# Triangle steps by a list of words, second residual in the accumulator, second norm's sums on ScalarE

## Chip, cores and metric

The kernel runs on one core of a Trainium2 chip. The metric is the device time of one execution in microseconds (us). TensorE is called PE in the profile, its weight load PEld, VectorE DVE, ScalarE ACT, GpSimd POOL, and the engine that issues most DMAs SP.

## The reference

Two layers on an input of 4 images with 64 x 64 tokens of 256 channels, all in fp32. The first is a self-attention over all 4096 tokens of an image. The second is a triangle attention, a norm, an MLP and a second norm. What the change touches is the second layer:

```python
def _L1_conv_ref(x_in, Wq, Wk, Wv1, Wv2, Wo, ln_agg_g, ln_agg_b, W1, b1, W2, b2, ln_out_g, ln_out_b):
    # ... q, k, v1, v2 = projections in 8 heads of 32
    scores = jnp.einsum('bilhd,bljhd->biljh', q, k) / np.sqrt(d_k)
    att = jax.nn.softmax(scores, axis=2)
    out = jnp.einsum('biljh,bilhd,bljhd->bijhd', att, v1, v2)
    attn_out = out.reshape(B, N, N, E) @ Wo
    h = x_in + attn_out
    h = _layer_norm(h, ln_agg_g, ln_agg_b)
    mlp = jax.nn.relu(h @ W1 + b1) @ W2 + b2
    h = mlp + h                                    # the second residual
    return _layer_norm(h, ln_out_g, ln_out_b)      # the second norm
```

## The kernel before

The program goes through the images one after the other. For each there is an attention stage, bound by TensorE, and a triangle stage of 32 steps. While the triangle stage of image b runs, the tokens of image b-1 (16 pieces of 256) are led through output projection, norm, MLP and norm: one piece per two steps. I call two steps and a piece a period. After the last image a tail does 15 pieces alone.

A step makes 8 products, some on DVE (`R`, three buffers) and some on POOL (`Rp`, two buffers), which TensorE sums into `acc`:

```python
def product(self, step, m):
    # ... npool(step) of the 8 products go to POOL: 3 in an even step, 2 in an odd one (b > 0)
    eng.tensor_tensor(R, src.unsqueeze(1).to_broadcast([P, D, N]), v2[:, h], ALU.mult)

def accumulate(self, step, m):
    for c in range(4):                             # four column groups of TensorE
        nc.tensor.matmul(acc[32 * c : 32 * c + 32, n % 2, :], w[:, n, c, 16 * h : 16 * h + 32],
                         R[:, ts(c, 8), :].rearrange("p d j -> p (d j)"), ...)
```

Second residual and second norm of a piece:

```python
def residue(self, tt):                             # POOL: z = h * gain + (shift + b2)
    h = self.h.pop(tt)
    z = self.z[tt] = work.tile([P, 2, C], F32, tag="s4", name="z")
    nc.gpsimd.tensor_tensor(z, h, lag_bc.unsqueeze(1).to_broadcast([P, 2, C]), ALU.mult)
    nc.gpsimd.tensor_tensor(z, z, lb2_bc.unsqueeze(1).to_broadcast([P, 2, C]), ALU.add)

def stats_o(self, tt):                             # DVE: add the MLP's output, then the statistics
    z = self.z[tt]
    nc.vector.tensor_tensor(z, self.zp.pop(tt), z, ALU.add)
    self.stats(z, 2)

def finish(self, tt, eng=nc.gpsimd):               # POOL: gain and shift of the second norm, store
    eng.tensor_tensor(z, z, log_bc.unsqueeze(1).to_broadcast([P, 2, C]), ALU.mult)
    eng.tensor_tensor(z, z, lob_bc.unsqueeze(1).to_broadcast([P, 2, C]), ALU.add)
    nc.sync.dma_start(...)
```

The order is a Python loop that writes one step after the other. Each engine runs its own queue in this order:

```python
for step in range(NSTEP):
    # ... (cut: conditions; loads, takes and stores of the step before)
    L.product(step, Q_[0]); L.product(step, D_[0])
    if odd: rest.polish(0 if odd_a else 2, 4, nc.gpsimd)
    if even_a: rest.heads(nxt, 0)
    L.accumulate(step, D_[0])
    next_weights()                                 # sums and weights of step + 1
    if odd_a: rest.affine_a(nxt)
    if odd: rest.affine_o(now)
    # ... (cut: products and sums between pieces of token work)
    if odd_a: rest.turn(nxt); rest.residue(nxt); mps = [rest.hidden(nxt, 0), rest.hidden(nxt, 1)]
    # ...
    if step % 2 == 0 and pair + 1 < NPAIR: L.scores(pair + 1, ig // 2)
    # ...
    if even: rest.stats_o(now); rest.roots(0 if even_a else 2, 4)
```

## Time and profile before

The median was 3938.9 us (3 runs). Stage borders are the first and last matmul into `acc`; the table is read from the busy times by stretch.

| part | us | PE busy | DVE | ACT | POOL |
|---|---|---|---|---|---|
| first triangle stage (no old tokens) | 430.6 | 383.8 | 394.6 | 236.4 | 396.9 |
| second | 489.5 | 451.6 | 452.1 | 258.7 | 461.2 |
| third | 490.8 | 453.0 | 452.3 | 258.9 | 461.2 |
| fourth (17 pieces) | 495.6 | 459.9 | 455.5 | 262.4 | 463.8 |
| tail | 174.2 | 153.9 | 108.3 | 81.1 | 76.0 |

The rest of the span of 3936.3 us are attention stages of 409 us, with some 38 us of start ahead of the first, and transitions of 43 to 46 us. No engine alone explains a triangle stage: three are busy 92 to 94% of it. Busy time of DVE and PE overlaps at instruction borders, so the prediction counts from start to next start ("by pace").

### The profile page before, as it was taken

To read this page: it belongs to the slowest core of one execution; us is meant where nothing else is said; L and a number is where in the kernel's file an instruction comes from. 1 tells how busy PE (TensorE), PEld (TensorE's weight loads), DVE (VectorE), ACT (ScalarE), POOL (GpSimd) and SP (SyncE) were. 2 spreads that over 40 slices of the span, in tenths; PEclk is the share of its full clock that TensorE was granted. 3 is DMA by queue.
4 is the path that set the end of the run, shared out by engine and by line. 5 is a ranking of instruction groups with operands and counts; after the bars stand their busy time and mean duration, and the time that the engine had idled before them with its cause. 6 is when DMAs were issued, how large, how long until landed. Compare 5 with 4: busy or idle time off the path is not lost.

```text
span 3936.3 us, 59354 instructions
## 1 busy us (share of the span) xinstructions
PE 3737.0 (95%) x23302; PEld 1742.6 (44%) x23302; DVE 2708.9 (69%) x2291; ACT 1814.4 (46%) x3775; POOL 1927.0 (49%) x1024
## 2 busy tenths in 40 slices
PE   9999998889999999998999999999899999999998
PEld 5444444433444444443344454444344444444376
DVE  4454499896444499998454459999644447999965
ACT  3333455554333455554333345555433335555544
POOL 4000098993000099998000049999500007999954
PEclk9999999999999999999999999999999999999999
DMA  4111445552111434323111154233211134331221
GB/s 119 50 51 48 116 139 137 136 144 96 49 51 51 121 74 91 84 53 87 52 51 46 54 131 93 55 85 74 75 48 47 49 99 103 84 85 45 53 70 50
DMA packets 439713, 309.38 MB, mean 79 GB/s; under 512 B 299328, under 2 KB 404544, under 8 KB 432128
## 3 DMA queue, kind: packets, MB, share of 16 engines
q1 hardware_dynamic: 419952, 291.12, 28.2%
q10 hardware_dynamic: 16240, 8.59, 0.8%
q0 software_dynamic: 3232, 5.78, 0.6%
q8 instruction: 186, 3.05, 0.3%
q14 instruction: 103, 0.84, 0.1%
HBM read 165.88 MB, written 139.46 MB: 78 GB/s over the span
## 4 chain that ended last, share of the span: by engine, by line
PE 72%; ACT 9%; DVE 6%; DMA 5%; POOL 3%; issue 3%; SPq 3%; ACTq 0%; POOLq 0%; DVEq 0%
PE o L432 24%; PE acc L808 12%; PE proj L489 8%; PE s L410 7%; PE mp L956 5%; PE zp L974 3%; DVE R L799 3%; PE sp L704 3%; PE v1p L514 3%; POOL Rp L799 2%; ACT S L714 2%; ACT ao L816 2%; SPq L823 2%; PE hp L863 2%; PE y L474 1%
## 5 line engine op out<-in xcount | busy, mean ns | idle before, releaser
L799 POOL TENSOR_TENSOR Rp<-attP,v 128x2048 f32<-128x2048 f32 x328 | 1490.1, 4569 | 449.9 <-DMA qk<-k 324.7
L799 DVE TENSOR_TENSOR R<-att,v 128x2048 f32<-128x2048 f32 x696 | 1547.3, 2273 | 95.4 <-PE acc L808 44.2
L439 DVE TENSOR_TENSOR esum<-esum,e 128x2048 f32<-128x2048 f32 x224 | 512.7, 2289 | 583.4 <-ACT e L421 580.5
L808 PE MATMUL acc<-R,wsel 128*32 128x512 f32 x5568 | 727.7, 605 | 64.3 <-DVE R L799 43.1
L421 ACT ACTIVATE e<-s 128x1024 f32<-128x1024 f32 x512 | 496.5, 1021 | 403.6 <-PE s L410 381.8
L902 POOL TENSOR_SCALAR nt<-mv 128x4 f32<-128x4 f32 (+1 forms) x51 | 9.9, 193 | 1283.6 <-DVE mv L880 1279.5
L816 ACT COPY ao<-acc 128x1024 f32<-128x1024 f32 x256 | 261.5, 1021 | 547.2 <-PE acc L808 436.2
L432 PE MATMUL o<-e,vlo 128*128 128x512 f32 x1024 | 473.7, 605 | 0.0
L432 PE MATMUL o<-e,vhi 128*128 128x512 f32 x1024 | 472.6, 605 | 0.0
L808 PE MATMUL acc<-Rp,wsel 128*32 128x512 f32 x2624 | 350.7, 610 | 35.1 <-POOL Rp L799 34.9
L808 PEld LDWEIGHTS acc<-R,wsel 128*32 128x32 f32 x5568 | 143.2, 109 | 396.0 <-issue 198.7
L432 PEld LDWEIGHTS o<-e,vlo 128*128 128x128 f32 x1024 | 184.0, 189 | 280.8 <-issue 280.8
L432 PEld LDWEIGHTS o<-e,vhi 128*128 128x128 f32 x1024 | 184.3, 189 | 279.7 <-issue 279.7
L410 PE MATMUL s<-gT,fT 32*128 32x512 f32 x2048 | 302.2, 640 | 4.8 <-ACT e L421 4.5
L956 PE MATMUL mp<-hT,w 128*128 128x256 f32 x1024 | 250.4, 390 | 39.6 <-ACT hT L936 39.6
L741 ACT ACTIVATE es<-S,rd 128x64 f32<-128x64 f32 x1024 | 258.4, 338 | 26.9 <-DVE rd L733 25.0
L451 DVE RECIPROCAL rec<-den 128x512 f32<-128x512 f32 x32 | 107.4, 3357 | 215.6 <-PE den L449 215.6
L974 PE MATMUL zp<-w,hid 128*128 128x256 f32 x1024 | 247.3, 387 | 2.9 <-ACT hid L963 2.9
L956 PEld LDWEIGHTS mp<-hT,w 128*128 128x128 f32 x1024 | 182.9, 189 | 117.4 <-ACT hT L936 57.8
L974 PEld LDWEIGHTS zp<-w,hid 128*128 128x128 f32 x1024 | 186.5, 191 | 67.5 <-issue 40.3
L501 ACT COPY st<-proj 128x512 f32<-128x512 f32 x104 | 60.9, 585 | 293.2 <-issue 165.9
L410 PEld LDWEIGHTS s<-gT,fT 32*128 32x128 f32 x2048 | 82.9, 182 | 193.7 <-issue 172.6
(153 smaller groups left out, 3795.3 us busy)
## 6 DMA issues: line engine op xcount, KB each, us to landing
v<-v2d SPq DMA_DIRECT2D x24, 1024.0 KB, 13.0
v1c<-v1d SPq DMA_DIRECT2D x128, 128.0 KB, 3.0
aT<-ao SPq DMA_DIRECT2D x1024, 16.0 KB, 1.9
A<-aT SPq DMA_DIRECT2D x256, 64.0 KB, 2.1
out_dram<-z SPq DMA_DIRECT2D x63, 256.0 KB, 2.2
y<-yT SPq DMA_DIRECT2D x56, 256.0 KB, 2.0
q<-st SPq DMA_DIRECT2D x56, 256.0 KB, 2.6
v1d<-st SPq DMA_DIRECT2D x56, 256.0 KB, 2.2
```

The costliest lines, as they stand in the source:

```text
L410: nc.tensor.matmul(s_ps[r // 2][:, r % 2, :], fT[rows, tt, ts(n, P)], gT[rows, ts(qb, QB)], start=True, stop=not safe,)
L421: nc.scalar.activation(e[g][:, 2 * j : 2 * j + 2, :], s_ps[j], AF.Exp)
L432: nc.tensor.matmul(o_ps[qb], F.v[tt][:, r * 4 + n, :], es[:, r, :], start=(k == 0 and r == 0), stop=(k == 7 and r == 3),)
L439: nc.vector.tensor_tensor(esum[qb], esum[qb], es, ALU.add)
L489: nc.tensor.matmul(ps, w[:, cc, rows], y(qb, cc), start=(cc == 0), stop=(cc == 1))
L514: nc.tensor.matmul(ps[:, ts(n, C)], y(qb, cc)[:, ts(m * 2 + n, P)], wv1_sb[:, cc, :], start=(cc == 0), stop=(cc == 1),)
L741: nc.scalar.mul(self.e[:, i, :], rows[:, i, :], rec[:, i : i + 1])
L799: eng.tensor_tensor(R, src.unsqueeze(1).to_broadcast([P, D, N]), v2[:, h], ALU.mult)
L808: nc.tensor.matmul(acc[32 * c : 32 * c + 32, n % 2, :], w[:, n, c, 16 * h : 16 * h + 32], R[:, ts(c, 8), :].rearrange("p d j -> p (d j)"), ...
L816: nc.scalar.copy(self.ao[step][:, ts(np, 2)].rearrange("p k d j -> p k (d j)"), acc)
L956: nc.tensor.matmul(self.mp[:, fc % 2, :], w1_sb[:, cc, ts(fc, P)], self.hT[tt][:, cc, :], start=(cc == 0), stop=(cc == 1),)
L974: nc.tensor.matmul(zp[:, n, :], self.hid[tt][:, fc, ts(n, P)], w2_sb[:, fc, :], start=(fc == 0), stop=(fc == 3),)
```

## The change

Three things are changed. The intent of the first is to take the second residual off POOL and DVE: TensorE transposes `h` anyway; a second copy of that transposed tile, with the shift and b2 in its bias, is transposed back by TensorE into the accumulator of the MLP's output. The second takes the second norm's statistics to ScalarE, whose activations can give a sum. The third writes the later triangle stages from a list of words; "/1" behind a word is by how many periods it is late, so what belongs to one step is spread over up to three periods. In a word, R is a product, A a sum into `acc`, T the copy of an accumulator, E and O the even and odd step.

```diff
+ORDER = """
+    r0/1 AO0/2 AO1/2 m1/1 RO4/2 RE5/1 SO/1 RO5/2 TO0/2 sp/1 AO4/2 AO6/2 r1/1 e0/1 e1/1 AO5/2 AE5/1 TO1/2
+    RE4/1 AE4/1 z0/1 WO/1 RE3/1 VO/1 fi/2 SE z1/1 tO/1 so/1 RE6/1 RE0/1 cO/1 sa AE3/1 RE7/1 RE2/1 AE6/1
+    AE2/1 AE0/1 rr/1 pp/1 WE RE1/1 AE7/1 AE1/1 fo/1 fa TE1/1 RO2/1 tE TE0/1 RO7/1 h1/-1 RO3/1 h0/-1 ht
+    RO6/1 hU AO3/1 hT AO2/1 AO7/1 RO1/1 cE RO0/1 m0 VE
+""".split()
 # ... (cut: dictionaries by step in place of single fields)
+        def sums_of(self, src, junk, mv, k):
+            for n in range(2):
+                nc.scalar.activation(
+                    junk[:, n, :], src[:, n, :], AF.Identity, scale=1.0 / (16 * C), accum_out=mv[:, k + n, 0:1]
+                )
+            for n in range(2):
+                nc.scalar.activation(
+                    junk[:, n, :], src[:, n, :], AF.Square, bias=mv[:, k + n, 0:1], scale=-1.0 / 16,
+                    accum_out=mv[:, k + n, 1:2],
+                )
+        def carried(self, tt):
+            self.h.pop(tt)
+            self.hT2[tt] = self.turned(tt, lab2_sb, tag="s4")
 # ... in outputs(), after the MLP's matmuls into zp:
+            if tt in self.hT2:
+                for cc in range(2):
+                    nc.tensor.matmul(
+                        zp[:, n, ts(cc, P)], self.hT2[tt][:, cc, ts(n, P)], ident,
+                        start=False, stop=(cc == 1), is_transpose=True,
+                    )
 # ... (cut) the tail: h and z of odd and even pieces in different buffers
-            self.h[tt] = work.tile([P, 2, C], F32, tag="h", name="h", bufs=1)
+                tag = "A" if far and tt % 2 else "h"
+                self.h[tt] = work.tile([P, 2, C], F32, tag=tag, name="h", bufs=1)
-            z = self.z[tt] = work.tile([P, 2, C], F32, tag="s4", name="z")
+            z = self.z[tt] = work.tile([P, 2, C], F32, tag=("s4", "es")[tt % 2], name="z")
 # ... (cut) next_layer1 walks the list:
+        for period in range(NP + 4):
+            for word, late in words:
+                i = period - int(late)
+                # ... of_step(word, i) or of_piece(word, i)
```

The first triangle stage keeps its old loop, but loads v1 after the stores of the step before, not ahead of them. The tail keeps POOL's residual and DVE's statistics; its last two half pieces are interleaved.

## The prediction

> **What bounds the kernel now.** I first read the busy time in stretches. The span of 3936.3 us falls into four rounds (one per image) of an attention stage, a triangle stage and a short transition, and then a tail; the stage borders are the first and last matmul into `acc`. The diff leaves the attention stages and the first triangle stage (430.6 us, it carries no tokens of an earlier image) as they are in substance. What it rewrites is the three other triangle stages, 489.5 + 490.8 + 495.6 = 1475.9 us, and, a little, the tail of 174.2 us. Columns: stretch, its length, then busy us of PE, PEld, DVE, ACT, POOL with instruction counts.
>
> ```profile
> 1376.15:1865.69 489.54, 451.64 (x3672) 208.17 (x3672) 452.09 (x377) 258.69 (x674) 461.17 (x254) 1.00 0.33 77
> 2320.71:2811.55 490.84, 453.00 (x3672) 208.19 (x3672) 452.32 (x377) 258.85 (x674) 461.17 (x254) 0.99 0.33 76
> 3762.07:3936.30 174.23, 153.89 (x738) 129.64 (x738) 108.33 (x370) 81.06 (x217) 76.03 (x60) 0.96 0.22 61
> ```
>
> In a triangle stage three engines are busy 92 to 94% at once; ScalarE only 53%. A stage has 32 steps, that is 16 periods of an even and an odd step with one piece of 256 tokens, so a period lasts 489.5/16 = 30.6 us. Next I read the groups of instructions of the second triangle stage for POOL and DVE.
>
> ```profile
> L799 POOL TENSOR_TENSOR Rp<-attP,v 128x2048 f32<-128x2048 f32 x80 | 363.6, 4564 | 30.3 <-PE acc L808 16.1 <-ACT attP L758 14.1
> L982 POOL TENSOR_TENSOR z<-z,log_bc 128x512 f32<-128x512 f32 x16 | 20.5, 1280 | 0.0
> L946 POOL TENSOR_TENSOR z<-z,lb_bc 128x512 f32<-128x512 f32 x15 | 19.2, 1282 | 1.2
> L945 POOL TENSOR_TENSOR z<-h,lag_bc 128x512 f32<-128x512 f32 x15 | 19.2, 1281 | 0.0
> ...
> L799 DVE TENSOR_TENSOR R<-att,v 128x2048 f32<-128x2048 f32 x175 | 388.5, 2271 | 12.8 <-ACT attP L758 7.0 <-PE acc L808 4.2 <-DMA v2d<-stage 1.6
> L879 DVE BATCH_NORM_STATS2 st<-z 128x6 f32<-128x256 f32 x32 | 13.2, 412 | 0.5
> L887 DVE TENSOR_TENSOR z<-zp,z 128x512 f32<-128x512 f32 x16 | 11.0, 689 | 19.8 <-issue 15.2 <-PE zp L974 3.3 <-POOL Rp L799 1.3
> ```
>
> POOL makes 5 of the 16 products of a period and DVE 11. From start to next start a POOL product takes 4.52 us and a DVE product 2.19 us. POOL per period is 5 x 4.52 = 22.6, the residual (two operations) 2.6, the last scaling of the output 2.6, the seven small operations of the norm 1.9: 29.7 us of 30.6. So **POOL is full to 97%**, and each wait on it lengthens the stage. The third view is the chain of waits through one period (start, us, what):
>
> ```profile
> 2590.87 2.02 PE mp L956 x8
> ...
> 2609.17 1.04 PE acc L808 x8
> ...
> 2610.27 1.02 ACT ao L816
> 2611.34 2.03 PE sp L704 x64
> 2613.39 2.09 ACT S L714 x2
> 2615.48 0.85 ACT ao L816
> 2616.33 1.90 ACT es L741 x8
> ...
> 2621.87 1.15 PE mp L956 x4
> ```
>
> From `mp` to the next `mp` it is 31.0 us: TensorE, then ScalarE's accumulator copy, the scores, their exponentials, the weights, the norm, and TensorE again. An in-order loop between TensorE and ScalarE is thus as long as POOL's own work. Either must be shortened together with the other for a gain.
>
> **What the Trainium skill says.** "Perfetto Trace Analysis", section Identifying the Most-Contended Engine, takes occupancy as a fair measure for Vector, Scalar and GPSIMD but not matmul busy time. The trace agrees: TensorE is busy 28.2 us per period, but paced from start to start (below) its work depends much on how often it changes kind. "GPSIMD Engine Reference", section 3.1, has 4497 ns on GPSIMD and 2293 ns on VectorE for a 2048-element fp32 tensor_tensor; the trace has 4564 and 2271, so work taken off POOL is worth what the rows say. [...]"ScalarE: Activation LUTs", section Table sets: the hidden batching unit, that cheap functions fill every set. If Square is one of them, as I assume, no table load (1.28 us, once in this trace) is added. The trace of before has neither a Square nor an accumulator output.
>
> **The change part by part,** per period.
> - *Residual on TensorE.* The two POOL operations on `h` go: -2.6 us. DVE's addition of `z` goes: -0.73 us. Added are two ScalarE activations of 128x256 (`hT` takes 0.46 each by pace: +0.9) and four TensorE transposes (0.109 each between equals: +0.44).
> - *Second norm's sums on ScalarE.* On DVE two BATCH_NORM_STATS2 (0.445 each by pace) and two aggregates (0.10) go: -1.1. ScalarE gets four activations of 128x256 at about 0.46 to 0.5: +1.9.
> - *Word list.* No work is added or removed; the order changes. The matmuls into `acc` come in four runs per period, where the trace shows 7.4. By pace a group of eight is 0.86 us inside a run; leaving a run costs 0.135 more, and entering it from `mp`, `zp` or `hp` 0.2. A period saves about 3.4 x 0.33 = 1.1 us of TensorE. And the loop is cut: what one period produces is used one or two periods later.
>
> New floors: **POOL** 29.7 - 2.6 = 27.1. **DVE** 11 x 2.19 = 24.1, sums 1.42, reciprocals 0.24, first norm 1.1: 26.9. **TensorE** with scores: `acc` 16 x 0.86 + 4 x 0.135 = 14.3, `sp` 1.9, `mp` 2 x 1.73 + 0.2, `zp` 3.46 + 0.44, `att` 1.0, `hp` 2.2, `htp` 0.5, entering 0.2: 27.6; without scores (about 4 of 16 periods) 25.7. **ScalarE** 16.2 + 2.8 = 19.0. Three engines stand within 0.7 us of each other, all below 28.
>
> The floor of a stage is 12 x 27.6 + 4 x 27.1 = 440 us. Three engines that all work at their floor can't be had in order and with two or three buffers for each product; before, the bound engine had 97%. The new order has at least one tight place: the path from `z1` by the sums, the roots, POOL's small operations and `fo` to the next `hp` is 2.0 + 0.5 + 1.9 + 1.0 us and four hand-overs, against some 6.4 us of other TensorE work placed there. I take 0.8 to 1.0 us of waits and choose a period of 28.4. The list is one to two periods deep, so it drains longer; I add 5 us. A stage then lasts 16 x 28.4 + 5 = 459, the last 464 as it carries one piece more. Saved: 30.5 + 31.8 + 31.6 = 94 us.
>
> *Tail.* Its period is 10.17 us, of which 9.5 are TensorE's by pace. It is held by another loop: POOL's last scaling, the output's landing, POOL writes the next `z`, ScalarE overwrites the single `h`. The change gives `z` and `h` a second name each. I count 14 x 0.5 = 7 us, and 2 us for the two halves of the last piece, which are now interleaved. Sum: 94 + 9 = 103, of which I take 101: 3938.9 - 101 = **3838 us**.
>
> **The rivals.**
> 1. *TensorE becomes the bound and gives the gain back.* For it: four transposes more, and its waits are only 38 us per stage already. If the runs save no switching, TensorE's floor is 28.7 and with the same 3% of waits the period 29.6: 474 + 5 per stage, some 40 us saved with the tail, 3900 us. Against it: the order visibly batches the `acc` groups.
> 2. *A new wait takes the place of the old.* A buffer in PSUM must stay for the second sum until `fo`, where before DVE's addition freed it at once; with the heads of the next piece held too, both buffers of that pool are taken, so TensorE may wait for POOL's in-order small operations. One wait of 1 us per period more costs 48 us: 3886.
> 3. *It runs almost at the floor,* as the list looks searched out to the instruction: 442 us per stage, 3790.
> 4. *ScalarE becomes the bound.* At 19 of 28 us I discount it, unless Square brings table loads: 2 x 1.28 us per piece would still leave it under 22.
>
> **Range and chances.** Faster by over 2% needs 3938.9/1.02 = 3861.7, a saving of 77 us: a period of at most 29 with tail and drain as above. Rivals 1 and 2 at full size miss that. I put 0.76 on faster, 0.22 on within 2%, 0.02 on slower, which would take waits of over 4 us in each period. The range is 3798 (rival 3 nearly) to 3884 (rival 2).
>
> **What would show each step.** In the later triangle stages POOL's rows for the residual and DVE's row for `z<-zp,z` are gone; ScalarE is busy about 300 us per stage; new transposes into `zp` have 4 per piece. Right: stages of 450 to 470 us with POOL and TensorE both above 93% of it, and waits of `acc` for `R` and `Rp` smaller. Tail about 165 us. Rival 1 shows as POOL and DVE waiting for PE `acc` with TensorE at 97%. Rival 2 shows as `hp` or `fo` waiting for POOL's `rn`. Wrong in the sizes: an accumulating activation much longer than 0.6 us, a table load per piece, or a drain much above 5 us. Attention stages stay at 409 us, the first triangle stage at 430; if those move I have misread the diff.

## The result, and the profile after

The changed kernel took 3815.05 us in the median (3813.3 to 3819.2, 4 runs), the kernel before 3938.7 in the same rounds. The ratio is 0.9688, with a 95% interval of 0.9672 to 0.9705. Ratios here are the mean time of one kernel's fast runs over that of the other's of the same rounds, so not quite the ratio of the medians. The prediction had 3838, with 3798 to 3884, and 0.76 on faster.

The busy times by stretch of the changed kernel: second and third triangle stage, and tail (stretch, length, then PE, PEld, DVE, ACT, POOL).

```profile
1384.82:1831.19 446.37, 432.66 (x3730) 224.30 (x3730) 422.29 (x294) 295.21 (x822) 420.43 (x223) 0.99 0.35 83
2288.41:2732.20 443.79, 431.05 (x3730) 223.99 (x3730) 422.22 (x294) 295.13 (x822) 420.52 (x223) 1.00 0.35 83
3640.52:3813.20 172.68, 150.40 (x730) 128.15 (x730) 120.86 (x364) 82.36 (x217) 75.63 (x60) 0.96 0.22 61
```

PE is now busy 97% of a stage, DVE and POOL 94 to 95%, ACT 66%. The three stages are shorter by 43.2, 47.0 and 43.9 us (the fourth lasts 451.7), 134 us together. Of it, 6.6 us are lost again: each later transition is 2.2 us longer (48.2 for 46.0). Half a piece's heads stood there before; the other half, 1.1 us of TensorE, has joined it, and the first `acc` matmul of the stage now waits 1.3 us, for POOL's first product, where it waited 0.2 us for one of DVE. The first triangle stage and the transition ahead of it are 5.5 and 1.2 us longer, and the tail only 1.5 us shorter. The spans differ by 123.1 us.

The chain of waits through one period of the third stage of the changed kernel (start, us, what):

```profile
2480.62 1.92 PE mp L1026 x8
2482.55 1.85 PE acc L843 x16
2484.40 1.93 PE mp L1026 x8
2486.33 1.91 PE sp L731 x64
2488.24 4.43 PE acc L843 x40
2492.67 1.93 PE zp L1046 x8
2494.59 0.22 PE zp L1052 x2
...
2497.19 5.29 PE acc L843 x48
...
2505.67 2.71 PE acc L843 x24
2508.39 0.63 PE mp L1026 x2
```

In the chain of before, ScalarE and TensorE took turns; here every link of the period is TensorE. From `mp` to `mp` it is 27.77 us, and the starts of the first norm's transposes lie 27.76 us apart ten times in a row. The `acc` matmuls come in four runs per period, where before there were seven to eight. The line of `zp L1052` is the new residual, 0.22 us twice.

What POOL and DVE have left, from the groups of instructions of the third stage:

```profile
L833 POOL TENSOR_TENSOR Rp<-attP,v 128x2048 f32<-128x2048 f32 x79 | 359.1, 4572 | 12.3 <-PE acc L843 12.3
L1060 POOL TENSOR_TENSOR z<-z,log_bc 128x512 f32<-128x512 f32 x16 | 20.6, 1289 | 0.0
...
L833 DVE TENSOR_TENSOR R<-att,v 128x2048 f32<-128x2048 f32 x174 | 386.9, 2274 | 17.4 <-PE acc L843 12.3 <-DMA v2d<-stage 5.1
```

The products and POOL's last scaling cost what they did; the rows of the residual on POOL and of DVE's addition and second statistics are gone. POOL's idle time in front of its products is 12 us, where it was 30.

What ScalarE got, from the groups of instructions of the third stage:

```profile
L998 ACT ACTIVATE hT<-htp,lab_sb,lag_sb 128x256 f32<-128x256 f32 x60 | 29.1, 567 | 9.4 <-PE htp L993 9.4
...
L937 ACT ACTIVATE z<-zp,mv 128x256 f32<-128x256 f32 x32 | 14.7, 469 | 0.0
L933 ACT ACTIVATE z<-zp 128x256 f32<-128x256 f32 x32 | 12.0, 375 | 36.1 <-PE zp L1052 33.8 <-PE att L785 2.3
L937 ACT ACTIVATION_READ_ACCUMULATOR z<-zp,mv 128x1 f32 x32 | 6.5, 203 | 0.0
L933 ACT ACTIVATION_READ_ACCUMULATOR z<-zp 128x1 f32 x32 | 6.3, 198 | 0.2
```

`hT` is computed 60 times where it was 30. The sums are 64 activations and 64 small instructions that read the accumulator. No table load was added. ScalarE rose by 36.3 us per stage, 2.3 per period.

### The profile page after: what moved, and what is told of

Its sections match the earlier page's. It is cut to its first block, busy times and chain, and to the rows that moved or that the text cites.

```text
span 3813.2 us, 60145 instructions
## 1 busy us (share of the span) xinstructions
PE 3683.6 (97%) x23498; PEld 1796.9 (47%) x23498; DVE 2641.8 (69%) x2050; ACT 1935.7 (51%) x4257; POOL 1804.3 (47%) x930
## 4 chain that ended last, share of the span: by engine, by line
PE 81%; POOL 7%; issue 3%; DMA 3%; DVE 3%; ACT 3%; SPq 0%; ACTq 0%; POOLq 0%; DVEq 0%
PE o L453 24%; PE acc L843 17%; PE proj L510 8%; PE s L431 7%; POOL Rp L833 6%; PE mp L1026 5%; PE zp L1046 5%; PE sp L731 3%; PE v1p L535 3%; PE hp L902 2%; PE y L495 2%; DVE R L833 1%; PE att L785 1%; ACT S L741 1%; PE den L470 1%
## 5 line engine op out<-in xcount | busy, mean ns | idle before, releaser
L833 DVE TENSOR_TENSOR R<-att,v 128x2048 f32<-128x2048 f32 x696 | 1548.9, 2274 | 113.7 <-PE acc L843 76.6
L460 DVE TENSOR_TENSOR esum<-esum,e 128x2048 f32<-128x2048 f32 x224 | 512.8, 2289 | 583.0 <-ACT e L442 579.8
L843 PE MATMUL acc<-R,wsel 128*32 128x512 f32 x5568 | 711.0, 605 | 44.2 <-DVE R L833 32.1
L843 PEld LDWEIGHTS acc<-R,wsel 128*32 128x32 f32 x5568 | 153.7, 110 | 381.5 <-issue 263.1
L843 PEld LDWEIGHTS acc<-Rp,wsel 128*32 128x32 f32 x2624 | 81.1, 111 | 211.7 <-issue 140.6
```

Of the source, the lines that this page charges most:

```text
L460: nc.vector.tensor_tensor(esum[qb], esum[qb], es, ALU.add)
```

## The experiments

Every kernel gave a right result. Stage lengths are those of the three later triangle stages in one profile; whole times are medians, with the ratio to the kernel before of the same rounds.

**1. Each part undone, in the list as it stands.** All variants are written into the code of the changed kernel.

`undo_residual`: residual on POOL, added on DVE, then ScalarE's sums.

```diff
-            self.hT2[tt] = self.turned(tt, lab2_sb, tag="s4")
+            self.residue(tt, "s4")
 # word "so":
+            nc.vector.tensor_tensor(z, self.zp.pop(tt), z, ALU.add)
+            self.sums_of(z, junk, self.mv, 2)
```

> The changed kernel with the second residual back on POOL (two operations per piece) and DVE's addition of it; word list and ScalarE's sums stay. Theory A (POOL's work sets the period as soon as the loop is cut): POOL's floor is again 29.7 us per period, so the three later triangle stages go from 444 to 452 us back to 478 to 490 and the whole to 3910 to 3935 us. Rival B (the order alone made the gain, POOL has slack): stages stay under 455 us and the whole under 3840.

`undo_sums`: the statistics back on DVE, from PSUM.

```diff
-                rest.sums_of(rest.zp[t0 + q], z, rest.mv, 2)
+                rest.stats(rest.zp[t0 + q], 2)
```

> The changed kernel with the second norm's statistics back on DVE (two BATCH_NORM_STATS2 and two aggregates per piece, read from PSUM). Theory A: DVE's floor goes from 26.9 to 28.0 us per period, 0.4 above TensorE's 27.6, so stages of 452 to 462 us and a whole of 3835 to 3865. Rival B (DVE has slack, the sums moved for nothing): within 8 us of 3815. Rival C (ScalarE's sums are a burden on the path to the next heads): faster than 3810.

`list_only`: both.

> Both changes of arithmetic undone, the word list alone. Theory A: POOL at 29.7 and DVE at 28.7 us per period bind, stages of 478 to 492 us, a whole of 3910 to 3940, so the list alone gives next to nothing. Rival B (order alone made the gain): under 3850.

Measured: 4070.9 us (1.0337), 4093.6 us (1.0396) and 4108.0 us (1.0432), stages of 529 to 547 us. All three are slower than the kernel before, which none of the theories had expected. What DVE waited for in the third stage of `undo_sums` (waiter, awaited: us in total, times, longest):

```profile
DVE st L918 <- PE zp L1057: 66.8, 16, 5.4
```

Sixteen times, once per period, DVE stands 4.2 us in front of the statistics until TensorE has finished `zp`. The word `so` stands where it suits ScalarE, which has time; on DVE it blocks all products behind it. TensorE waits for these products in turn:

```profile
PE acc L843 <- DVE R L833: 73.1, 19, 4.5
```

And the granted clock, the last figure but two of the stage's busy times, falls to 0.93, from 1.00 in the changed kernel:

```profile
2380.71:2920.14 539.43, 464.29 (x3730) 229.02 (x3730) 440.64 (x358) 268.42 (x694) 421.93 (x223) 0.93 0.29 68
```

The wait has a second cost. A group of four `acc` matmuls starts 0.41 us after the one before it in the changed kernel. In `undo_sums` TensorE is idle for 3.4 to 4.5 us once per period, and in all 16 periods of the third stage three to seven groups behind this gap start 0.81 to 0.84 us apart, half the pace, before 0.41 returns. A period with scores lasts 34.16 us for 27.76; of these 6.4 us the gap makes 4.7 and the slow groups typically 1.6.

So these three runs say nothing of the size of the parts. They say that an in-order list holds for its own work only: 1.1 us of work per period given to another engine, in the place that it had, made a stage 90 to 96 us longer.

**2. The same with the word moved.** In the two `_late` variants `so` stands two DVE products later, just ahead of the roots.

```diff
-    ... tO/1 so/1 RE6/1 ... AE2/1 AE0/1 rr/1 pp/1 ...
+    ... tO/1 RE6/1 ... AE2/1 AE0/1 so/1 rr/1 pp/1 ...
```

> As undo_sums (second norm's statistics on DVE), but with their word set two VectorE products later in the list, just ahead of the roots. In undo_sums DVE stood 67 us per stage in front of the statistics, waiting for the piece's last matmul into zp, since a word that is harmless on ScalarE blocks DVE's queue. Theory A (1.1 us more work on DVE per period, no block): stages of 450 to 465 us, a whole of 3830 to 3870. Rival (the sums have to be on ScalarE for the order to work at all): stages stay above 500 us, over 4000.

> The word list alone (residual on POOL, addition and statistics on DVE), with DVE's word at the later place. Theory A: POOL's 29.7 and DVE's 28.7 us of work per period set the stage: 480 to 495 us, a whole of 3915 to 3945, about the kernel before. Rival: the list alone makes most of the gain, stages under 460 us. Third: the place still blocks an engine, over 500 us.

Measured: `undo_sums_late` 3833.2 us (0.9741), stages 452.9, 450.9 and 456.4; `list_only_late` 3912.0 us (0.9939, the same within 2%), stages 478.7, 477.0 and 481.6. In the third stage DVE no longer waits for `zp` in `undo_sums_late`, and once, for 1.4 us, in `list_only_late`. The stages of both fall into what theory A expected, or up to 3 us below; the whole of `list_only_late` came 3 us under its range. A period with scores of `list_only_late` lasts 29.9 us, near the 29.7 us that the prediction summed for POOL, and in most of them TensorE stands 1.7 us in front of a product of POOL: with the list alone it is POOL that binds. (`undo_residual` was not run again with a later place; the residual's share comes from these two.) With the place right, having the sums on ScalarE is worth 18 us over the three stages (against the changed kernel's 446.4, 443.8 and 451.7); the wrong place cost 84 to 89 us in each stage.

**3. The order undone.** Both changes of arithmetic in the old loop of one step after the other.

```diff
-                    next_layer1(b, L, rest, ahead, F)
+                    old_layer1(b, L, rest, ahead, F)     # the loop of before, with carried() and sums_of()
```

> Both changes of arithmetic in the old order of one step at a time. Theory A: the loop between TensorE and ScalarE of 31.0 us stays, with ScalarE's additional 2.8 us partly in it: stages of 485 to 505 us, a whole of 3920 to 3975. Rival B (POOL's work alone set the period before): stages of 450 to 465 us, a whole of 3815 to 3850.

Measured: 3952.4 us (1.0038), stages 489.6, 491.0 and 498.2, where before had 489.5, 490.8 and 495.6. The lengths are those of theory A. POOL's work fell to 423 us per stage, near the changed kernel's 421, and the stage did not move: in the old order the two changes of arithmetic together are worth nothing. What less work on POOL alone would give there is not shown. ScalarE's sums stand in the loop between TensorE and ScalarE in this run's chain of waits, 1.9 us between the `acc` matmuls and the taking of the scores (`S`):

```profile
2620.91 0.39 ACT z L929
...
2621.31 0.56 ACT z L929 x3
...
2622.13 0.66 ACT z L933 x3
```

The first ten periods of the third stage last 31.3 us on average where before had 30.8. So part of what POOL's relief could have given may have been lost to the longer loop; a run with the residual alone in the old order would tell, and there is none.

`all_undone` is the control for this: all three parts undone within the same code, the load order of the first stage too.

> Control: residual on POOL, statistics on DVE, old order in the later triangle stages and old load order in the first, all within the code of the changed kernel (only the changed tail stays). If the variants are sound, its later triangle stages are those of before, 488 to 497 us, and the whole is 3930 to 3945. The first triangle stage: 430 to 432 us would say that its 4 to 6 us in the other runs come from the rewritten code, 434 to 437 again, with an order of instructions equal to before, that they are not of the order at all.

Measured: 3940.9 us (1.0011), stages 493.8, 489.6 and 489.2. The frame is sound; and the fourth stage, 6 us shorter than in the profile of before, and the second, 4 us longer, show how far single stages vary. I rest nothing on differences of that size in one stage.

**4. What binds now.** Three runs give the changed kernel more work on one engine and nothing else.

`more_pool` does the two operations of `finish` twice in the first three images (with a gain of one and a shift of zero the result stays): 2.6 us per period, what the change took from POOL.

```diff
-            eng.tensor_tensor(z, z, log_bc.unsqueeze(1).to_broadcast([P, 2, C]), ALU.mult)
+            for again in range(2 if tt // NP < 3 else 1):
+                eng.tensor_tensor(z, z, log_bc.unsqueeze(1).to_broadcast([P, 2, C]), ALU.mult)
 # and so for the addition of lob_bc
```

> The changed kernel with the two operations that finish a piece of the first three images done twice on POOL, so that POOL has again 2.6 us more per period, its work of before, and nothing else moves (with a scale of one and a shift of zero the result stays right). Theory A: POOL binds again, stages of 478 to 490 us, a whole of 3910 to 3945. Rival (POOL has slack): under 3840.

Measured: 3911.6 us (0.9935), stages 480.1, 476.4 and 480.9. That is 95 us more in the stages for 48 x 2.6 = 125 us of work. TensorE's largest wait in the third stage is the one that theory A names:

```profile
PE acc L843 <- POOL Rp L833: 25.0, 19, 2.1
```

`more_dve` repeats one reduction of 0.71 us per period, `more_pe` does the first norm's four transposes three times in 42 pieces (0.87 us each).

```diff
+            for again in range(2 if self.b > 0 and step % 2 == 0 else 1):
                 nc.vector.tensor_reduce(den, rows, AX.X, ALU.add)
```

```diff
+            for again in range(3 if tt % NP > 1 and tt // NP < 3 else 1):
                 for cc in range(2):
                     for n in range(2):
                         nc.tensor.transpose(htp[:, cc, ts(n, P)], h[:, n, ts(cc, P)], ident)
```

> The changed kernel with one 0.71 us reduction per period repeated on DVE (48 times, 34 us in all). If DVE binds with the others: 3835 to 3850. If TensorE alone binds and DVE has the 0.7 us of slack that the floors gave it: 3815 to 3828.

> The changed kernel with the four transposes of the first norm done three times into the same place, in 42 pieces: 0.87 us more of TensorE in a period, 36.6 us in all; the result stays right. If TensorE sets the period: 3843 to 3858. If it has slack: under 3828.

Measured: `more_dve` 3819.4 us (0.9701), stages together 3.6 us longer for 34 us of work; `more_pe` 3843.9 us (0.9758), stages together 25 us longer for 36.6 us. By period the answer is sharper: with the additional transposes a period with scores of the third stage lasts 28.64 us for 27.76, so all of their 0.87 us appears, and the periods without scores stay as they were (27.0 and 27.1 us for 26.8 and 27.2). TensorE sets the periods with scores; DVE has the 0.7 us of slack that the floors gave it. POOL has about half a microsecond: of its 2.6 us more, 2.0 appear in the period.

**5. The first triangle stage.** The prediction had it unchanged; it was 5.5 us longer.

```diff
 # first_layer1, at the head of the step; fetches() has it no more
+            L.fetch_v1(step + 2)
             if scored:
                 L.take_scores()
```

> The changed kernel with the loads of v1 in the first triangle stage again ahead of the stores of the step before, as the old order had them. Theory: the stage's 5.5 us more are this order of the load queue (the load of the next image waits behind them), so the first triangle stage goes from 436.1 to 430 to 432 us and the whole to about 3810. Rival (chance or the late allocation of the accumulator's copy): no change of over 1 us.

Measured: 3816.8 us (0.9689), the stage 434.4 us. The theory falls: the order of the loads is worth at most 2 us, and not even that is shown, as two runs without this edit have 434.3 us, too (`undo_sums_late`, `more_pool`). In this run the queues of SP, ACT, POOL and DVE have, instruction for instruction, the order of before, and the time is lost at the steps in which the 1 MB loads of v2 start, where TensorE waits for the load of the next image (8.6 us in all, 6.4 before), and 1.5 us in the first step. In `all_undone`, with the same order again, the stage was 436.6. The profile of before, a single one, had 430.6. The whole times point to a real difference: the 12 runs of `all_undone` have a median 4.6 us above the 15 of the kernel before in the same rounds (interval of the ratio 1.0002 to 1.0020), though in the two profiles its later stages are 3 us shorter together. Where these 4 to 6 us come from stays open; it is 0.15% of the time.

**6. The tail.** It was to gain 9 us and gained 1.5. DVE and POOL in one period of the changed kernel's tail, in order of time:

```profile
3728.34 1.26 POOL L1061 TENSOR_TENSOR z<-z,lob_bc 128x512 f32<-128x512 f32 x1
...
3728.47 1.15 DVE L956 TENSOR_TENSOR nt<-nt 128x2 f32<-128x2 f32 x1
3729.56 1.27 POOL L1017 TENSOR_TENSOR z<-h,lag_bc 128x512 f32<-128x512 f32 x1
...
3729.65 1.20 DVE L957 TENSOR_SCALAR nt<-nt 128x2 f32<-128x2 f32 x1
...
3730.89 0.16 DVE L960 TENSOR_TENSOR rn<-nt,rs 128x2 f32<-128x2 f32 x1
3730.90 1.28 POOL L1018 TENSOR_TENSOR z<-z,lb_bc 128x512 f32<-128x512 f32 x1
3731.08 1.12 DVE L961 TENSOR_TENSOR rn<-mv,rn 128x2 f32<-128x2 f32 x1
```

An operation of DVE on two columns takes 0.16 us, or 1.12 to 1.20 when POOL runs, and then it ends within 0.02 us of POOL's. The Trainium skill's "SBUF — State Buffer", section SBUF: two separate sides, says that VectorE and GpSimd share a port pair as an exclusive lock, held for the whole instruction, in which the other is fully blocked, and that it concerns VectorE's operations in a 2-port mode or with two SBUF inputs, the latter only against a GpSimd operation that reads SBUF, as these do. This trace agrees for the operations with two inputs; the one held `TENSOR_SCALAR` has a single tile as input, and whether it ran in a 2-port mode the trace doesn't show. The large products of DVE, with one input from PSUM, are not touched: 2274 ns, as long as the pure SBUF additions of the attention stages, where POOL is idle (2289).

`tail_dve` takes the residual of the tail from POOL to DVE.

```diff
-        def residue(self, tt):
+        def residue(self, tt, eng=nc.gpsimd):
 # ...
-                self.residue(tt)
+                self.residue(tt, V)
```

> The changed kernel with the tail's residual (two operations per piece) on DVE in place of POOL. Theory: in the tail DVE's small operations, 0.16 us alone, end only when a running POOL operation ends (1.15 to 1.20 us), three times per piece, and this makes the period 10.33 us; with two POOL operations fewer a piece takes 9.6 to 10.0 us, the tail 160 to 168 us in place of 172.7, the whole 3803 to 3811. Rival (a chain of latencies through ScalarE holds the tail, the holding-up is harmless): DVE's 1.4 us more make it the same or slower, 3815 to 3830.

Measured: 3805.5 us (0.9660), the fastest of all; the tail 160.2 us, a piece 9.51 us, TensorE's own pace, twelve times in a row. DVE's chain of small operations in its tail:

```profile
3713.37 0.16 DVE L956 TENSOR_TENSOR nt<-nt 128x2 f32<-128x2 f32 x1
3713.57 0.17 DVE L957 TENSOR_SCALAR nt<-nt 128x2 f32<-128x2 f32 x1
3713.77 0.16 DVE L960 TENSOR_TENSOR rn<-nt,rs 128x2 f32<-128x2 f32 x1
3713.97 0.16 DVE L961 TENSOR_TENSOR rn<-mv,rn 128x2 f32<-128x2 f32 x1
```

DVE got two operations more per piece (1.4 us at the 0.69 us that such an addition takes alone) and the tail got shorter. Two of POOL's operations are gone, and the small operations start later, behind DVE's own residual, when POOL's last scaling has ended; so they run undisturbed. DVE's busy time in the tail even fell, from 120.9 to 115.4 us. The version with the list and this tail beats the kernel before by 3.4% and, by the two ratios, the changed one by 0.3%.

## Why the prediction was right, and where it was not

The direction, the range and the mechanism hold; the gain was 22% larger than predicted (123.7 us for 101). The whole came nearer than its terms: the stages gave 134 us for 94, the tail 1.5 for 9, and some 13 us were lost where the prediction had no term (transitions 6.6, first stage 5.5, the transition ahead of it 1.2). That these offset each other was luck.

- **The loop and POOL bound together: shown, but for the old loop by itself.** New arithmetic alone moves the three stages from 1476 to 1479 us (`undo_list`), the list alone to 1437 (`list_only_late`), list and residual to 1360 (`undo_sums_late`), all three to 1342. So of 134 us the list gives 39, the residual on top of it 77, the sums on top of both 18. The parts are not to be added in another order: without the list the other two together are worth nothing. With the list alone POOL binds (29.9 us per period). With the arithmetic alone a loop binds that has the sums in it; that the old loop without them would have held the stage just so was read from the chain, not tested.
- **The floors: right.** TensorE's 27.6 us per period became 27.76 in periods with scores. The periods without, for which POOL's 27.1 was entered, measure 26.8, 27.2 and 25.4 in the third stage. DVE's slack of 0.7 us was confirmed by `more_dve`, ScalarE's 19.0 us is 18.4 (295 / 16).
- **The switching of TensorE: right in sum, misread in its place.** Four runs of `acc` per period were read out of the list and are in the trace, and a run costs 0.34 us beyond its matmuls, as the prediction had it (0.135 + 0.2). But it had 0.135 for leaving a run and 0.2 for entering it. From start to start some 0.22 us lie at the end of a run (to the next kind 0.52 us in place of 0.41, and that kind's first matmul 0.32 in place of 0.22) and 0.12 at its start (0.31 in place of 0.22, then 0.43 in place of 0.41). The Trainium skill's "TensorEngine Tiling (Array Packing)", section Key Properties, says that a change of tiling mode drains TensorE; the traces agree and give these sizes.
- **The term that was mis-sized: "I take 0.8 to 1.0 us of waits and choose a period of 28.4".** In the periods with scores the waits measured 0.2 us or less (27.76 us for a floor of 27.6). The profile lists 13.8 us of waits of TensorE for the third stage, 0.9 per period on average, but they lie at its start (6.5 us, up to its first two runs of scores) and behind its last scores. The "tight place" from `z1` to the next `hp` cost TensorE 0.4 us at `hp` and 1.0 at `htp` in the whole third stage. A stage of 16 x 28.4 + 5 = 459 was therefore 444 to 446. I had put near-floor running under the rivals (rival 3, 442 us per stage) though I wrote that the list looked searched out to the instruction. The drain of 5 us was not measured apart: start, drain and waits together put the second and third stage 6 and 4 us above the floor of 440.
- **Rivals.** TensorE did become the bound (rival 1), but at the floor that the working gave it and not at 29.6. Rival 2, a wait for POOL's `rn`, is in the trace at ScalarE (9.9 us in the third stage), which has time for it. Rival 4 is out.
- **The tail: wrong step.** "It is held by another loop [...] The change gives `z` and `h` a second name each. I count 14 x 0.5 = 7 us". The buffers did break that loop (POOL's wait for the output's landing, 33.2 us in the tail before, is gone), but POOL's residual then ran directly behind its scaling and, together with the scaling, held DVE's small operations three times per piece: 10.33 us per piece for 10.17. `tail_dve` shows that without two of POOL's operations the 9.51 us are reached. The trace of before had the sign, which I had passed over, in the order of time of its tail:

```profile
3830.96 1.27 POOL L983 TENSOR_TENSOR z<-z,lob_bc 128x512 f32<-128x512 f32 x1
3831.10 1.15 DVE L904 TENSOR_TENSOR nt<-nt 128x2 f32<-128x2 f32 x1
```

  A two-column operation of DVE took 1.15 us there, too, and ended with POOL's.
- **Transitions and first stage:** 2.2 us each, for half a piece's heads that moved and a wait for POOL's first product, which I had not entered, and 5.5 us that stay open.

## What to carry to other kernels

Where several engines are all above 90% and the chain of waits runs through two of them in turn, less work or a new order may help little alone (here 0 and 39 of 134 us); compute the floor of each engine by start-to-start pace, and expect that a well searched order can run within 1 to 2% of the highest. A list of words in order belongs to the engines that it was made for: move an operation to another engine and its place has to be looked for again, or one blocked queue can cost five times the work that was moved (here 84 to 89 us against 18 us per stage), in part because TensorE ran at half pace for some time behind each long gap. And keep small VectorE operations on a critical chain apart in time from GpSimd's.

## What the Trainium skill lacked or had wrong

- No page names what follows each ACTIVATE with an accumulator output on ScalarE; it would belong to "ScalarE: Activation LUTs". The ACTIVATE itself takes what it takes without that output (469 ns with a bias tile, where the MLP's, with a bias tile too, takes 472, 128x256), but each comes with an ACTIVATION_READ_ACCUMULATOR of 198 to 203 ns, about 0.09 us by pace.
- "TensorEngine Tiling (Array Packing)" has the drain at a change of mode but no size: here 0.12 us on entering a run of 128x32 matmuls from full-array matmuls and 0.22 us on leaving it for them, some 2.5 us per period in the kernel before (an estimate, from 7.4 runs per period).
- "SBUF — State Buffer" has the shared lock right; that it reaches a two-column operation (0.16 to 1.2 us) on a chain of norms, three times per piece, and that the tail went from 172.7 to 160.2 us when two of POOL's operations left, are this case's figures.
